# A planned instruction order with a reserve on VectorE's results and TensorE's operands

## The chip, the cores and the metric

The kernel runs on one core of a Trainium2 chip. The metric is the device time in microseconds of one execution; for the kernel before it is the median of three runs. A profiled execution gives the trace from which the views below come. The engines are named as the profile does: PE is TensorE (PEld its weight loads), DVE VectorE, ACT ScalarE, POOL GpSimd, SP SyncE, which issues nearly all transfers (SPq is its queue).

## What is computed

Four graph layers are applied to 32 independent graphs ("batches" in the kernel) of 512 nodes with 128 features, all in float32. Each layer normalizes x, applies a ReLU and adds a graph layer's result to x:

```python
h = jnp.maximum(_layernorm(x), 0.0);  x = x + L0(h, adj)   # degree-normalized aggregation, leaky relu
h = jnp.maximum(_layernorm(x), 0.0);  x = x + L1(h, adj)   # elu of three projections, aggregations by adj and its transpose, tanh
h = jnp.maximum(_layernorm(x), 0.0);  x = x + L2(h, adj)   # four inner layers with L2-normalized adj in both directions, tanh
h = jnp.maximum(_layernorm(x), 0.0);  x = x + L3(h, adj)   # message passing and a GRU cell
```

So each batch is a long chain of small matmuls with vector and scalar work between them, and the batches do not depend on each other.

## The kernel before

The kernel first records every operation of all 32 batches with an engine, an expected duration, what it reads and what it writes. Then a planner, at build time, plays the recorded operations through in order of expected time and so fixes for each engine the order in which its instructions are issued. On the chip each engine runs its list strictly in that order and waits where an operand has not arrived. The planner's view of how late a result is:

```python
class Plan:
    SIGNAL = {"PE": 0.2, "DVE": 0.13, "ACT": 0.14, "POOL": 0.06, "SP": 0.05, "AQ": 0.05}
    RESULT = {"PE": 0.0, "DVE": 0.125, "ACT": 0.13, "POOL": 0.05}
    LOAD = 0.1
    RATE, ALONE, TRANSFER, ISSUE = 400.0, 175.0, 1.5, 0.45
    ...
    def lag(self, o, n):          # from the start of o until n, which needs it, may start
        queued = o.engine == n.engine and o.engine in self.RESULT
        if queued:
            return o.us + self.RESULT[o.engine]
        return o.us + o.land + self.SIGNAL[o.engine] + self.LOAD * (n.engine == "PE")
```

`order()` keeps a ready queue for each engine. Of the ready operations it takes the one with the smallest key, a due time of its batch (batches are due `PERIOD` = 27 apart) less the length of the chain that still follows it. An operation that needs a buffer is held while too few are free, and newer batches have to leave some for older ones:

```python
new = [x for x in item[1].bufs if x.slot is None and x.kind in free]
older = item[1].batch - min(unfinished)
if any(len(free[x.kind]) < len([y for y in new if y.kind == x.kind])
       + older * self.kept.get(x.kind, 0) for x in new):
    held.append(item)
    continue
...
event(now + o.us + o.land + self.SIGNAL[e], "end", o)      # o's buffers may be given on
```

The kinds of buffers are "bank" (PSUM banks), "s2" (512 columns), "s4" and "s8"; the last argument says how many of each kind stay free for each older batch:

```python
plan = Plan(sb, psum, {"bank": 8, "s2": 32, "s4": 6, "s8": 10}, {"bank": 1, "s2": 6, "s4": 0, "s8": 1})
```

Loads of adjacency matrices and of x are marked `yields`: they are not issued while a turn through DRAM is under way.

Where the planner sees TensorE idle for longer than 0.7 us, filler products (`ps_idle`, 128 columns, results unused) are put in, `n = int(min(gap, cold) / COLD + max(gap - cold - 0.1, 0.0) / WARM)` of them with `COLD` = 0.428 and `WARM` = 0.2225; `cold` is spent in the first gap.

The operations that the text below names by their line of the kernel before (the lines of the changed kernel are one higher):

```python
# L530  x of a batch is loaded, 256 KB; L527 halves of adj (a) and its transpose (aT), 512 KB each
# L537, L539, L540  layernorm statistics of x (bn, mv, v) on DVE; L579 their power on POOL;
#                   L587 nb on DVE; L591 h = relu(...) on ACT, in four chunks
# L600 a [128, 512] matrix is transposed in 32x32 blocks (blk) on DVE;
# L609 four stores of 64 KB to DRAM (turn_...); L613 one load of 256 KB back (turned, or f4r);
# L633 ACT copies the turned matrix into place (hT, f); L899 DVE adds f4r to x
# L346 every ordinary product; L711 the products of seven() (ps_seven)
# L667 sd = products + bias on DVE; L689, L724, L737 the sums and differences around seven() on DVE
# L752, L832 row sums of a and sums of squares of a and aT on ACT
# L783 z from the first layer's products on DVE
# L805, L806, L808 rep = elu(...): exp on ACT, then two steps on DVE
# L854 a and aT are scaled by rows of norms on DVE (8 of 512 columns each batch)
# L883 f = tanh(...) on ACT, after each inner layer;  L957 the result is stored, 256 KB
aggregate(psi, rep, 0, aT)       # rep is the weight operand of the product with aT and with a
```

A matmul of n columns in the program appears as two records in the trace; `ps_t` transposes as one.

Of the kernel before, what the change touches and what calls it, by code (L numbers as in the profile page):

```python
# [96 lines left out]
class Plan:  # L97
# [2 lines left out]

    SIGNAL = {"PE": 0.2, "DVE": 0.13, "ACT": 0.14, "POOL": 0.06, "SP": 0.05, "AQ": 0.05}
    RESULT = {"PE": 0.0, "DVE": 0.125, "ACT": 0.13, "POOL": 0.05}

    LOAD = 0.1

# [51 lines left out]
    def lag(self, o, n):  # L161
# [6 lines that stand above are left out]
    def order(self):  # L168
# [13 lines left out]
        for o in self.ops:  # L182
            unfinished[o.batch] = unfinished.get(o.batch, 0) + 1
        queues, idle_at = {e: [] for e in self.SIGNAL}, dict.fromkeys(self.SIGNAL, 0.0)
        under_way = 0
        events, seq = [], 0

        def event(at, what, o=None):
            nonlocal seq
            seq += 1  # L190
            heapq.heappush(events, (at, seq, what, o))
# [5 lines left out]
        while events:  # L197
# [14 lines left out]
            for e, queue in queues.items():  # L212
# [24 lines left out]
                event(now + o.us, "idle")  # L237
                event(now + o.us + o.land + self.SIGNAL[e], "end", o)
                for n in o.next:
# [36 lines left out]
def gnn_stack(  # L276
# [13 lines left out]
    sb = ctx.enter_context(tc.tile_pool(name="sb", bufs=1))  # L290
    psum = ctx.enter_context(tc.tile_pool(name="psum", bufs=1, space=bass.MemoryType.PSUM))
    dram = ctx.enter_context(tc.tile_pool(name="dram", bufs=1, space=bass.MemoryType.DRAM))
    plan = Plan(sb, psum, {"bank": 8, "s2": 32, "s4": 6, "s8": 10}, {"bank": 1, "s2": 6, "s4": 0, "s8": 1})

    w_sb = const.tile([P, W_COLS], F32, name="w_sb")
    c_sb = const.tile([P, C_COLS], F32, name="c_sb")
# [716 lines left out]
```

## Time and profile before

| | |
|---|---|
| median of 3 runs | 2313.61 us (2312.37 to 2313.68) |
| span of the profiled execution | 2312.6 us, 28086 instructions |
| mean granted TensorE clock | 1.000 |
| DMA | 200.82 MB in 132334 packets, mean 87 GB/s |
| median time to landing: x, 256 KB | 5.3 us |
| median time to landing: half of aT, 512 KB | 5.2 us |
| median time to landing: stores of a turn, 64 KB; load back, 256 KB | 1.8 us; 2.7 us |

The page gives, for each engine, busy time with its share of the span and the number of instructions. In a view in order of time a line has start, duration, engine, source line, operation, output and inputs, shape and count, and in brackets the idle time of the engine before it and what ended it. In a view of waits a line has who waited for whom, the total in us, how many times, and the longest. Ends of matmuls are modelled, and matmuls are pipelined.

### The profile page before, as it was taken

The page shows a single profiled execution, that of the slowest core. Times are in us where ns is not written, and L with a number is a line of the kernel's source. Part 1 is how long each engine was busy: PE and PEld are TensorE (multiplying, and loading weights), DVE is VectorE, ACT ScalarE, POOL GpSimd, SP SyncE. Part 2 cuts the span into 40 slices and gives each one's busy share as a digit, 9 for nine tenths or more (in the row PEclk, how much of TensorE's full clock was granted, in tenths as well). Part 3 has the DMA queues.
Part 4 walks back from the last instruction along what each step waited for, and adds up shares of the span by engine and source line. Part 5 has one row for each costly group of instructions (what it writes and reads, how often), then busy time and mean ns, then how long its engine had stood idle before and what let it go on. Part 6 is the DMA issues. An engine that isn't in the chain of part 4 may idle for free.

```text
span 2312.6 us, 28086 instructions
## 1 busy us (share of the span) xinstructions
PE 2300.3 (99%) x9674; PEld 1448.6 (63%) x9674; DVE 1530.9 (66%) x4179; ACT 905.0 (39%) x1929; POOL 235.1 (10%) x171
## 2 busy tenths in 40 slices
PE   9999999999999999999999999999999999999999
PEld 7656666566666666666666656666566666666656
DVE  6646666677666776667766667766677666766656
ACT  7313434424344353433433434344343434434312
POOL 2000110101101011100101011010110101001100
PEclk9999999999999999999999999999999999999999
DMA  7001322323223232233232232222332322323201
GB/s 262 28 28 60 118 83 73 101 68 125 71 76 110 73 111 82 75 99 100 83 92 73 91 101 87 87 91 74 100 92 82 101 69 96 110 64 107 90 10 33
DMA packets 132334, 200.82 MB, mean 87 GB/s; under 512 B 18912, under 2 KB 79072, under 8 KB 132192
## 3 DMA queue, kind: packets, MB, share of 16 engines
q1 hardware_dynamic: 131904, 198.91, 27.2%
q8 instruction: 76, 1.25, 0.2%
q14 instruction: 66, 0.54, 0.1%
q10 hardware_dynamic: 288, 0.13, 0.0%
HBM read 160.05 MB, written 38.93 MB: 86 GB/s over the span
## 4 chain that ended last, share of the span: by engine, by line
PE 91%; DMA 4%; DVE 3%; SPq 0%; POOL 0%; ACT 0%; issue 0%; ACTq 0%; POOLq 0%
PE ps_agg L346 61%; PE ps_seven L711 11%; PE ps_sd L346 9%; PE ps_upd L346 4%; PE ps_gate L346 3%; DMA x<-in_x 1%; PE ps_msg L346 1%; PE ps_node L346 1%; PE ps_lin L346 1%; DMA turn_f4r<-blk 1%; DMA a<-in_adj 0%; DMA f4r<-turn_f4r 0%; POOL sc L579 0%; DVE blk L600 0%; DMA bounce<-inv 0%; DVE g L934 0%
## 5 line engine op out<-in xcount | busy, mean ns | idle before, releaser
L346 PE MATMUL ps_agg<-aT,sd 128*128 128x512 f32 x1024 | 505.5, 593 | 0.0
L346 PE MATMUL ps_agg<-a,sd 128*128 128x512 f32 x1024 | 492.8, 594 | 1.1 <-DVE sd L689 0.9
L579 POOL TENSOR_TENSOR sc<-v,neg_half 128x4 f32<-128x4 f32 (+1 forms) x127 | 176.5, 1390 | 1671.7 <-DVE v L540 1270.0
L591 ACT ACTIVATE h<-xr,nb,sc 128x128 f32<-128x128 f32 x384 | 158.3, 482 | 298.2 <-DVE nb L587 297.7
L346 PEld LDWEIGHTS ps_agg<-a,sd 128*128 128x128 f32 x1024 | 179.0, 191 | 149.6 <-issue 145.4
L346 PEld LDWEIGHTS ps_agg<-aT,sd 128*128 128x128 f32 x1024 | 181.5, 191 | 110.5 <-issue 102.0
L711 PEld LDWEIGHTS ps_seven<-t_sb,s 128*128 128x128 f32 x1140 | 168.8, 191 | 102.6 <-issue 89.7
L346 PE MATMUL ps_agg<-f,w_sb 128*128 128x512 f32 x448 | 230.2, 595 | 0.0
L346 PE MATMUL ps_sd<-w_sb,f 128*128 128x256 f32 x768 | 223.0, 380 | 0.0
L346 PEld LDWEIGHTS ps_sd<-w_sb,f 128*128 128x128 f32 x768 | 137.5, 191 | 115.5 <-issue 95.2
L711 PE MATMUL ps_seven<-t_sb,s 128*128 128x128 f32 x1140 | 178.4, 275 | 1.2 <-DVE s L689 1.2
L883 ACT ACTIVATE f<-ps_agg,cf_sb 128x512 f32<-128x512 f32 x128 | 87.5, 683 | 186.8 <-PE ps_agg L346 186.6
L667 DVE TENSOR_TENSOR sd<-ps_sd,rf_sb 128x512 f32<-128x512 f32 x128 | 87.6, 684 | 85.7 <-PE ps_sd L346 84.3
L346 PE MATMUL ps_agg<-aT,rep 128*128 128x512 f32 x256 | 131.4, 595 | 4.0 <-DVE rep L808 4.0
L346 PE MATMUL ps_agg<-a,rep 128*128 128x512 f32 x256 | 130.7, 592 | 0.0
L346 PE MATMUL ps_agg<-aT,msg 128*128 128x512 f32 (+1 forms) x264 | 130.1, 579 | 0.0
L711 PEld LDWEIGHTS ps_seven<-w_sb,f 128*128 128x128 f32 x512 | 77.0, 191 | 39.8 <-issue 32.5
L346 PE MATMUL ps_agg<-aT,h 128*128 128x256 f32 (+2 forms) x384 | 99.4, 381 | 0.6 <-ACT h L564 0.6
L346 PEld LDWEIGHTS ps_agg<-f,w_sb 128*128 128x128 f32 x448 | 77.9, 191 | 35.0 <-issue 29.7
L667 DVE TENSOR_TENSOR sd<-ps_sd,sd 128x512 f32<-128x512 f32 x64 | 43.7, 683 | 84.7 <-PE ps_sd L346 84.7
L832 ACT ACTIVATE sq<-aT 128x512 f32<-128x512 f32 x128 | 80.4, 628 | 35.9 <-DMA aT<-in_adjt 33.5
L737 DVE TENSOR_TENSOR ev<-ps_seven,ev 128x512 f32<-128x512 f32 x95 | 64.3, 677 | 44.4 <-PE ps_seven L711 44.2
(168 smaller groups left out, 3733.9 us busy)
## 6 DMA issues: line engine op xcount, KB each, us to landing
aT<-in_adjt SPq DMA_DIRECT2D x124, 512.0 KB, 5.2
a<-in_adj SPq DMA_DIRECT2D x62, 512.0 KB, 5.1
turn_turned<-blk SPq DMA_DIRECT2D x348, 64.0 KB, 1.8
turned<-turn_turned SPq DMA_DIRECT2D x87, 256.0 KB, 2.7
spaced<-bounce SPq DMA_DIRECT2D x32, 512.0 KB, 3.6
x<-in_x SPq DMA_DIRECT2D x32, 256.0 KB, 5.3
out<-xo SPq DMA_DIRECT2D x31, 256.0 KB, 2.1
turn_f4r<-blk SPq DMA_DIRECT2D x116, 64.0 KB, 1.8
```

What stands on the lines that cost most here:

```text
L346: op("PE", t_mm(n), lambda: nc.tensor.matmul(out_of(ps.ap()), lhs(), rhs(), start=start, stop=stop), reads, [ps], later=later)
L579: op("POOL", t_pow(n), lambda: nc.gpsimd.tensor_tensor(inv.ap()[:, :n], v8.ap()[:, :n], neg_half[:, :n], op=ALU.pow), [v8, NH], [(inv, {0})])
L591: op("ACT", t_act(D, 2), lambda c=c: nc.scalar.activation(h.ap()[:, c, :], xin.ap()[:, c, :], AF.Relu, bias=nb.ap()[:, c:c + 1], scale=inv ...
L667: op("DVE", t_tt(N), lambda ps=ps, h=h: nc.vector.tensor_add(sd.ap()[:, 2 * h:2 * h + 2, :], ps.ap().rearrange("p (j v) -> p j v", j=2), s ...
L711: op("PE", t_mm(D), lambda j=j: nc.tensor.matmul(ps.ap()[:, k * H + j * D:k * H + (j + 1) * D], lhs()[:, j * P:(j + 1) * P], rhs(), start= ...
L737: op("DVE", t_tt(N), lambda: nc.vector.tensor_add(ev.ap(), bank_b.ap()[:, None, :H].to_broadcast([P, 2, H]), ev.ap()), [bank_b, ev], [ev])
L832: op("ACT", 0.73, lambda c=c, s=s, m=m: nc.scalar.activation(sq.ap(), m.ap()[:, c, :], AF.Square, accum_out=stat.ap()[:, s * NC + c:s * NC ...
L883: op("ACT", t_act(N, 1), lambda ps=ps, i=i, f_new=f_new: nc.scalar.activation(f_new.ap(), ps.ap(), AF.Tanh, bias=cf_sb[:, i:i + 1]), [ps, ...
```

## The change

When the planner fixes the order, a result of DVE counts as seen by the other engines 0.25 us after its end instead of 0.13, and an operand of a matmul that comes from another engine or a transfer counts 0.25 us later instead of 0.1. Both are later than the results arrive, so that the order has a reserve where an instruction takes longer than the planner thought. With it the number of "s2" buffers that a newer batch leaves free for each older one goes from 6 to 5. The instructions themselves, their operands' shapes and the filler rule are the same; only the order, the buffers' places and the number of fillers can differ.

```diff
-    SIGNAL = {"PE": 0.2, "DVE": 0.13, "ACT": 0.14, "POOL": 0.06, "SP": 0.05, "AQ": 0.05}
+    SIGNAL = {"PE": 0.2, "DVE": 0.25, "ACT": 0.14, "POOL": 0.06, "SP": 0.05, "AQ": 0.05}
     RESULT = {"PE": 0.0, "DVE": 0.125, "ACT": 0.13, "POOL": 0.05}
 
-    LOAD = 0.1
+    LOAD = 0.25
...
-    plan = Plan(sb, psum, {"bank": 8, "s2": 32, "s4": 6, "s8": 10}, {"bank": 1, "s2": 6, "s4": 0, "s8": 1})
+    plan = Plan(sb, psum, {"bank": 8, "s2": 32, "s4": 6, "s8": 10}, {"bank": 1, "s2": 5, "s4": 0, "s8": 1})
```

## Prediction

> **What bounds the kernel now.** I read the page's busy times first, then TensorE's waits, then the waits of the engine that is named there, then single places in order of time. The page's first part:
>
> ```profile
> PE 2300.3 (99%) x9674; PEld 1448.6 (63%) x9674; DVE 1530.9 (66%) x4179; ACT 905.0 (39%) x1929; POOL 235.1 (10%) x171
> ```
>
> TensorE bounds, but its 99% hides how much is left. In order of time, its matmuls of 512 columns look like this:
>
> ```profile
> 1000.42 1.02 PE L346 MATMUL ps_agg<-a,rep 128*128 128x512 f32 x2
> 1001.28 1.02 PE L346 MATMUL ps_agg<-aT,sd 128*128 128x512 f32 x2
> ```
>
> Two records (one product in the program) start 0.86 us before the next two and are drawn 1.02 us long. So a record overlaps its successor by some 0.16 us, and a stall shows only with what exceeds that. I therefore counted from start to start. The spacing of records that wait for nothing is 0.429 us at 512 columns (3322 records), 0.324 at 384 (128), 0.216 at 256 (1188) and 0.112 at 128 (5027): 1425 + 41 + 257 + 563 = 2286 us. From the first start (1.4 us) to the last there are 2308 us, so 21 us are stalls; another 3 us follow the last matmul. Of the 2286, 9.6 us are the 86 filler records (43 filler products). So 2277 us are real work that the change leaves alone, and all it can win lies in 21 + 10 us.
>
> Where the 21 us are, by the matmul's last-arriving operand: 6.5 us lie in the first 50 us, 14.5 net in the rest, nearly none in the last 100. TensorE's waits name the cause:
>
> ```profile
> PE ps_agg L346 <- DVE rep L808: 4.0, 6, 0.9
> PE ps_seven L711 <- DVE s L689: 1.2, 3, 0.7
> PE ps_agg L346 <- DVE sd L689: 0.9, 4, 0.2
> ```
>
> Start to start, after the first 50 us: L808 4.4 us at 6 places, L689 5.2 us at 21, the tanh of L883 1.5 us at 13 (0.12 each), hT (L633) 0.5 us at 2: 11.6 us. The other 4.4 us are steps of about 0.1 us with no late operand.
>
> Why is VectorE late? Its own waits, and one place of each kind:
>
> ```profile
> DVE xr L899 <- DMA f4r<-turn_f4r: 17.5, 14, 2.5
> DVE bn L537 <- DMA x<-in_x: 10.3, 10, 3.7
> ```
>
> ```profile
> 1421.65 0.29 DVE L537 BATCH_NORM_STATS2 bn<-x 128x6 f32<-128x128 f32 x1 [1.13 <-DMA x<-in_x]
> 1421.86 0.67 DVE L808 TENSOR_TENSOR rep<-rep,sd 128x512 f32<-128x512 f32 x1
> ```
>
> ```profile
> 1422.68 1.10 PE L346 MATMUL ps_agg<-aT,rep 128*128 128x512 f32 x2 [0.94 <-DVE rep L808]
> ```
>
> A statistic of the next x stands in VectorE's queue ahead of rep; x has not landed; rep waits behind it, and TensorE with it. The other kind is a late f4r (the matrix turned through DRAM):
>
> ```profile
> 1625.50 0.69 DVE L899 TENSOR_TENSOR xr<-xr,f4r 128x512 f32<-128x512 f32 x1 [2.48 <-DMA f4r<-turn_f4r]
> ```
>
> ```profile
> 1628.94 0.94 PE L711 MATMUL ps_seven<-t_sb,s 128*128 128x128 f32 x6 [0.68 <-DVE s L689]
> ```
>
> So the named releaser is VectorE, but behind both kinds stands a transfer.
>
> **What the Trainium skill says.** "Perfetto Trace Analysis", section "Identifying the Most-Contended Engine": matmul busy share is a poor measure of the distance to the limit; the overlap above agrees. The same page, "DVE / Act Engine Instruction": the end shown is the write's acknowledgement, and the semaphore must still spread. Here stalled matmuls start 0.055 us after the end shown for L689's results and 0.147 us after L808's. Section "Tensor Engine Instruction" calls VectorE a strict FIFO: the x place agrees. "TensorE: Matmul & The Clock Gate", "What's actually happening": TensorE is throttled after idling some 3.4 us. The granted clock is 1.000 here and the longest stall 1.1 us, so no speed is at stake.
>
> **The change part by part.** No matmul, VectorE or ScalarE instruction changes its work. In the planner, a result of VectorE counts as seen 0.12 us later by every other engine, and any operand of a matmul from another engine or a DMA 0.15 us later (so VectorE to TensorE 0.27 us); and a newer batch need leave only 5 small buffers per older batch. Only orders move, so I read both orders, and for each matmul that waits I counted the matmul time (spacings above) between the matmul that feeds the VectorE or ScalarE work and this one, less that work's own durations (0.687 us for L667 from the trace, and so on). What is left must pay the hand-overs:
> - L808 to the aggregate: 15 of 63 places had 0.51 us or less. After: one in the first batch at 0.15, all others 0.76 or more, mostly 1.41.
> - L667 to the aggregate: 40 of 190 had 0.34 to 0.39; after, all but one have 0.65 or more.
> - L689 to the aggregate: least 0.49, a quarter below 0.78; after 0.72 and 1.01.
> - L883's tanh to the next product: 43 of 63 had about 0.4; after 0.63 at least.
>
> Two distances between issue and use matter more. x's load stood 2.6 to 2.8 us of matmul time ahead of its statistics, while the page has 5.3 us to landing; after, 9.4 us. f4r: from the VectorE transposition to its use 7.15 or 7.38 us; measured it needs 6.7 to 8.4; after, 9.13. The order also settles differently: before, it repeats every two batches (141.2 us of matmul time), after, every batch (70.65).
>
> Removed: L808 4.4 + L689 5.2 + L883 1.5 + L633 0.5 = 11.6 us. The 4.4 us of small steps stay.
>
> Added, fillers: 49 products instead of 43. Six by 0.223 us (two records of 0.112) is 1.3 us. Two of them stand before products in the first 42 us that wait anyway (0.5 to 0.75 us of stall behind the fillers), and cost nothing. The other four are new, near 250 us, where a tanh has too little beside it: 0.9 us.
>
> Added, transfers: the tightest path is now h1 turned through DRAM. From transposition to the product that uses hT the order leaves 7.45 us in every batch (before 7.41 and 7.67 in turn). Measured: 6.5 to 6.8 us until ScalarE starts its copy when nothing interferes, 0.62 us of copy, 0.06 us of hand-over: 7.2 to 7.5. And in the new order f4r's way back and the output store are issued just ahead of its way back, 256 KB each. The data of 256 KB take about 1.1 us on the queue alone and some 0.7 us in a busy stretch, so I allow 0 to 0.3 us of stall a batch, 0.1 on average: 27 x 0.1 = 2.7 us. For what I overlook in start and end, 1 us.
>
> Sum: 2313.6 - 11.6 + 0.9 + 2.7 + 1.0 = 2306.6. I say 2306.5 us, a gain of 0.3%.
>
> **Rivals.** (1) The reserve moves nothing that matters, because matmul work sets the cadence in both orders (141.2 us for two batches, 70.65 for one): 2314 us, with the fillers. For it speaks the 99%; against it that both transfers behind the stalls get 2 to 7 us more time. (2) The transfers gathered in one window become a stall in every batch. A period of one batch means that a site 0.5 us short costs 27 x 0.5 = 13 us, more than all that is won: 2317 us. For it speaks hT at 7.45 against 7.2 to 7.5, and from the first issue of a to the first product of h, 13.1 us, where the trace has h ready at about 12.0 to 13.0; against it, that in the old order 7.41 us for hT cost only 0.5 us in all. (3) All late operands vanish and nothing takes their place: 2313.6 - 11.6 + 0.9 = 2303 us; if the small steps went too, 2299.
>
> **Range and chances.** The floor of 2299 and rival (2) bound it. I hold the gain likelier than not, rival (2) in full at a tenth: 2299 to 2313 us. Two per cent is 46 us. All stalls and fillers together are 31, so faster by over 2% is excluded by the sum (0.01 for a mistake in it); slower by as much needs 1.7 us more stall in each of 27 batches (0.01).
>
> **What would show it.** In the changed profile: 98 filler records; TensorE's waits on L808 under 1 us in all, on L689 under 1 us; VectorE's wait for x nearly gone and for f4r under 5 us instead of 17.5; 2277 us of real work as before; any new wait should be on ScalarE's hT (L634 there), once in each batch. I am wrong if L808 and L689 still cost over 4 us start to start though x and f4r are early (then VectorE's queue, not the transfers, made them late), or if hT or h costs over 0.3 us in most batches.

## The result, and the profile after

The changed kernel takes 2325.86 us (median; 2321.68 to 2331.6), the kernel before, run beside it on the same chip, 2313.64 us (2311.85 to 2315.32). The ratio is 1.0054, with a 95% interval of 1.0040 to 1.0068: the change costs 12 us where the prediction had a gain of 7, and the time lies outside its range of 2299 to 2313 us.

The profiled execution of the changed kernel is its fastest: its span is 2319.9 us against 2312.6 before. So the trace shows 7.3 us of the 12, and the rest has to be read from the experiments. First the page's busy times, after:

```profile
PE 2298.2 (99%) x9686; PEld 1448.7 (62%) x9686; DVE 1521.4 (66%) x4179; ACT 898.9 (39%) x1929; POOL 206.5 (9%) x171
```

TensorE's busy time is lower than before (2300.3) although the kernel is slower, and 99% says nothing again. The chain of work that ended last says more; here its line of shares by engine, before and then after:

```profile
PE 91%; DMA 4%; DVE 3%; SPq 0%; POOL 0%; ACT 0%; issue 0%; ACTq 0%; POOLq 0%
```

```profile
PE 81%; DVE 7%; DMA 6%; ACT 3%; issue 2%; SPq 1%; POOL 0%; ACTq 0%; DVEq 0%
```

Ten points of the chain have left TensorE for other engines, transfers and the queue. TensorE's waits after (who waited for whom, total us, times, longest):

```profile
PE ps_sd L347 <- ACT hT L634: 15.2, 20, 1.4
PE ps_idle L963 <- POOL ident masks.py:199: 1.4, 1, 1.4
PE ps_agg L347 <- ACT h L565: 0.6, 1, 0.6
PE ps_agg L347 <- DVE diag L764: 0.5, 1, 0.5
PE ps_agg L347 <- DVE sd L668: 0.2, 1, 0.2
```

The three groups behind VectorE's rep and s have vanished, and one new group stands in their place: the products that use h1 turned (hT) wait for ScalarE's copy of it. VectorE's waits for transfers changed as follows:

```profile
DVE diag L764 <- DMA aT<-in_adjt: 35.7, 29, 2.1
DVE bn L538 <- DMA x<-in_x: 4.4, 2, 3.7
DVE xr L900 <- DMA f4r<-turn_f4r: 0.7, 2, 0.5
```

f4r fell from 17.5 us to 0.7, x from 10.3 to 4.4, of which 3.7 are the very first load. The new wait for aT (in nearly every batch) reaches TensorE only once, with 0.5 us (0.4 before).

Start to start, as the prediction counts, the books are these. Spacing without stalls: 2286.8 us before, 2288.2 after (12 more filler records). Stalls, net: 21.1 before, 27.0 after. Another 4.7 us lie ahead of the first product and behind the last in both, and the sums are the two spans, 2312.6 and 2319.9. Of the 27.0 us, 19.2 stand behind hT at 24 places, 0.8 us each; before it was 0.5 us. Everything else fell from 20.6 to 7.8.

One such place. The queue of SyncE in order of time, first the kernel before, then after (start, duration, what is issued):

```profile
1408.25 0.40 SPq L957 DMA_DIRECT2D out<-xo  x1
1409.66 0.34 SPq L613 DMA_DIRECT2D f4r<-turn_f4r  x1
1410.06 1.85 SPq L609 DMA_DIRECT2D turn_turned<-blk  x4
1413.82 0.34 SPq L613 DMA_DIRECT2D turned<-turn_turned  x1
```

```profile
1412.61 1.76 SPq L610 DMA_DIRECT2D turn_turned<-blk  x4
1414.60 0.34 SPq L614 DMA_DIRECT2D f4r<-turn_f4r  x1
1414.99 0.42 SPq L958 DMA_DIRECT2D out<-xo  x1
1415.80 0.32 SPq L614 DMA_DIRECT2D turned<-turn_turned  x1
1416.17 0.97 SPq L528 DMA_DIRECT2D aT<-in_adjt  x2
```

Before, the result's store and f4r's way back went out 5.6 and 4.2 us ahead of h1's way back. After, all three go out within 1.2 us. ScalarE and TensorE at the same place:

```profile
1420.81 0.62 ACT L634 COPY hT<-turned 128x512 f32<-128x512 f32 x1 [7.12 <-DMA turned<-turn_turned]
```

```profile
1421.48 1.78 PE L347 MATMUL ps_sd<-w_sb,hT 128*128 128x256 f32 x7 [1.07 <-ACT hT L634]
```

From the issue of the way back (1415.80) to the copy it is 5.0 us. Over the 25 batches in the middle the median is 4.53 us; before it was 2.62. The store itself takes longer as well (median us from issue to landing, last column, before and after):

```profile
out<-xo SPq DMA_DIRECT2D x31, 256.0 KB, 2.1
```

```profile
out<-xo SPq DMA_DIRECT2D x31, 256.0 KB, 3.2
```

### The profile page after: what moved, and what is told of

It reads as the page before. It is cut to its first block, busy times and chain, and to the rows that moved or that the text cites. A ratio compares the mean times of both kernels' runs of the same rounds, so it can differ in the third digit from the quotient of the medians.

```text
span 2319.9 us, 28193 instructions
## 1 busy us (share of the span) xinstructions
PE 2298.2 (99%) x9686; PEld 1448.7 (62%) x9686; DVE 1521.4 (66%) x4179; ACT 898.9 (39%) x1929; POOL 206.5 (9%) x171
## 4 chain that ended last, share of the span: by engine, by line
PE 81%; DVE 7%; DMA 6%; ACT 3%; issue 2%; SPq 1%; POOL 0%; ACTq 0%; DVEq 0%
PE ps_agg L347 55%; PE ps_sd L347 9%; PE ps_seven L712 9%; DMA turned<-turn_turned 4%; PE ps_upd L347 4%; DMA turn_turned<-blk 2%; ACT h L592 1%; PE ps_gate L347 1%; PE ps_msg L347 1%; PE ps_node L347 1%; PE ps_lin L347 1%; SPq L610 1%; DVE g L935 1%; DVE bn L538 1%; DVE blk L601 1%
## 5 line engine op out<-in xcount | busy, mean ns | idle before, releaser
L347 PE MATMUL ps_agg<-aT,sd 128*128 128x512 f32 x1024 | 492.6, 592 | 0.2 <-DVE sd L668 0.2
L347 PE MATMUL ps_agg<-a,sd 128*128 128x512 f32 x1024 | 485.8, 593 | 0.0
L580 POOL TENSOR_TENSOR sc<-v,neg_half 128x4 f32<-128x4 f32 (+1 forms) x127 | 149.1, 1174 | 1816.0 <-DVE v L541 1340.3
L347 PEld LDWEIGHTS ps_agg<-aT,sd 128*128 128x128 f32 x1024 | 186.8, 190 | 155.6 <-issue 142.8
L347 PE MATMUL ps_sd<-w_sb,f 128*128 128x256 f32 x768 | 217.8, 380 | 0.0
L712 PEld LDWEIGHTS ps_seven<-t_sb,s 128*128 128x128 f32 x1140 | 158.7, 191 | 50.3 <-issue 34.2
L712 PE MATMUL ps_seven<-t_sb,s 128*128 128x128 f32 x1140 | 166.3, 275 | 0.0
L634 ACT COPY hT<-turned 128x512 f32<-128x512 f32 x58 | 35.9, 618 | 193.6 <-DMA turned<-turn_turned 193.0
L920 ACT ACTIVATE mT<-ps_agg 128x512 f32<-128x512 f32 x31 | 18.5, 596 | 218.9 <-PE ps_agg L347 218.9
L855 DVE TENSOR_TENSOR a<-a,rows 128x512 f32<-128x512 f32 x128 | 86.1, 674 | 6.8 <-PE ps_agg L347 6.8
```

Of the source, the lines that this page charges most:

```text
L347: op("PE", t_mm(n), lambda: nc.tensor.matmul(out_of(ps.ap()), lhs(), rhs(), start=start, stop=stop), reads, [ps], later=later)
L580: op("POOL", t_pow(n), lambda: nc.gpsimd.tensor_tensor(inv.ap()[:, :n], v8.ap()[:, :n], neg_half[:, :n], op=ALU.pow), [v8, NH], [(inv, {0})])
L634: op("ACT", t_act(N), lambda: nc.scalar.copy(hT.ap().rearrange("p (c a r) -> p c a r", c=NC, a=NC), turned_cols(t)), [t], [hT])
L712: op("PE", t_mm(D), lambda j=j: nc.tensor.matmul(ps.ap()[:, k * H + j * D:k * H + (j + 1) * D], lhs()[:, j * P:(j + 1) * P], rhs(), start= ...
L855: op("DVE", t_tt(N), lambda m=m, c=c, s=s: nc.vector.tensor_mul(m.ap()[:, c, :], m.ap()[:, c, :], rows.ap()[:, s, :]), [(m, {c}), rows], [ ...
```

## The experiments

In all tables "way" is the median from the issue of h1's way back to the start of ScalarE's copy in the 25 middle batches, "stalls of hT" what TensorE loses there start to start (with the number of places), and "all" the net stalls of the whole span. Source lines in the profiles shift with the edits.

### Which of the two transfers does it

The changed kernel's orders are kept, and in the 25 batches single transfers are moved in SyncE's queue (the edit in short, not its code):

```diff
+ for back in ways_back_of_h1:                 # with f4r's way back and the store just ahead of it
+     for o in (the two transfers ahead):
+         if kind(o) in which:                 # e1: the store; e2: f4r's way back; e3: both
+             move o directly behind back
```

> The changed kernel with one thing moved: in the transfers' queue the store of the result (256 KB) goes behind the way back of h1's turn (256 KB) instead of ahead of it, in the 25 batches where both f4r's way back and this store stand ahead of it. All other engines' orders are the same. Theory A (transfers queue up: each of the two 256 KB ahead costs hT about 0.9 us): hT's way from issue to copy falls from 4.5 to about 3.6 us, TensorE's stalls for hT from 19 us to under 4 us, time about 2310 us. Rival B (the store alone does it, a write to DRAM in front of a read): way falls to 2.7 us, stalls to nothing, about 2306 us. Rival C (the loads of aT and x issued right behind take the bandwidth): way stays over 4.2 us, time stays about 2325 us.

> The changed kernel with f4r's way back moved behind h1's way back, the store stays ahead. Theory A: hT's way about 3.6 us, stalls for hT under 4 us, about 2310 us, as with the store moved. Rival B (the store alone): no gain, 2325 us. Rival C (the loads behind): 2325 us. f4r itself is about 1 us later, which its 9.1 us of room should bear: VectorE's wait for it under 10 us in all.

> The changed kernel with both f4r's way back and the store moved behind h1's way back. Theory A: hT's way 2.7 us, no stalls for hT beyond 1 us in all, time 2306 us (2313.6 less the 11.6 us of stalls that the new order removed, plus the fillers, plus what f4r's delay costs), so faster than the kernel before. Rival B: the same as with the store moved alone. Rival C: still 2325 us.

| run | ahead of h1's way back | way | stalls of hT | all | time | ratio (95%) |
|---|---|---|---|---|---|---|
| after | f4r, store | 4.53 | 18.7 (23) | 27.0 | 2325.86 | 1.0054 (1.0040 to 1.0068) |
| e1 | f4r | 3.38 | 4.3 (3) | 11.6 | 2304.94 | 0.9966 (0.9954 to 0.9978) |
| e2 | store | 2.75 | 0.7 (2) | 29.7 | 2323.84 | 1.0048 (1.0033 to 1.0063) |
| e3 | nothing | 2.67 | 1.0 (2) | 32.4 | 2324.81 | 1.0053 (1.0038 to 1.0068) |

Moving the store alone turns a loss of 12 us into a gain of 8. Moving f4r's way back frees hT even more (2.75 us), but then f4r itself is late: VectorE's wait for it was expected under 10 us and is 42.8. The waits of e2, VectorE's and TensorE's:

```profile
DVE xr L914 <- DMA f4r<-turn_f4r: 42.8, 26, 2.9
```

```profile
PE ps_agg L360 <- DVE rep L823: 14.9, 25, 1.2
```

This is the mechanism that the prediction had found in the kernel before (a late transfer holds up VectorE's queue, and TensorE with it), now in nearly every batch; there a late f4r stood before s, here it stands before rep. e3 goes the same way: f4r 44.9 us, rep 16.8 in 25 places. Two transfers want the same place in the queue, and the one sent behind pays. What was expected of each alone did not come: neither an equal share for the two nor "the store alone" describes 0.1 for the store, 0.7 for f4r and 1.9 for both. That transfers issued behind the way back slow it by themselves is refuted: with f4r and the store directly behind it (e3) it took 2.67 us, and the changed kernel's turns of h3, with nothing near them, 2.65. Whether the two halves of aT, 0.37 us behind, add to the delay of a way back that has f4r and the store ahead was not tested.

### The planner does it itself, and the queue it goes through

One word in the changed kernel has the store wait while a turn is under way (e5); or the store is issued from ScalarE's queue instead of SyncE's (e7):

```diff
- op("SP", 0.4, lambda: nc.sync.dma_start(out[b], xo.ap()), [xo], [], kb=256)
+ op("SP", 0.4, lambda: nc.sync.dma_start(out[b], xo.ap()), [xo], [], kb=256, yields=True)    # e5
+ op("SP", 0.4, lambda: nc.scalar.dma_start(out[b], xo.ap()), [xo], [], kb=256)               # e7
```

> The changed kernel with one word more: the store of the result is also held back while a turn through DRAM is under way. The order stays that of the changed kernel but for the store, which now stands behind h1's way back, and 45 of 4867 matmuls near the end. Theory (two 256 KB transfers ahead of hT's way back cost it 1.8 us, f4r's alone 0.7, which the order can bear): as with the store moved by hand, 2305 us, within 3; stalls for hT under 5 us. Rival (the gain of the store moved by hand was a chance of that one program): over 2312 us.

> The changed kernel with the store of the result issued from ScalarE's queue at the same place in the order, so that it isn't in SyncE's queue ahead of hT's way back. Theory (SyncE's queue hands its transfers' data on in turn, so what counts is what stands ahead in that queue): hT's way back falls to about 3.4 us as with the store moved behind it, stalls under 6 us, about 2306 us. Rival (the data paths are shared by all queues, whatever the queue): the way stays over 4.2 us and the time about 2325 us.

| run | way | stalls of hT | all | time | ratio (95%) |
|---|---|---|---|---|---|
| e5 | 3.39 | 2.8 (4) | 10.0 | 2304.39 | 0.9952 (0.9940 to 0.9964) |
| e7 | 4.79 | 25.8 (25) | 35.6 | 2329.18 | 1.0060 (1.0046 to 1.0074) |

e5 is faster than both kernels and has the lowest median here, though e1 (2304.94) and e14 below (2304.87) lie within the noise of it; its chain has 96% on TensorE. e7 shows that the harm is not done in SyncE's queue: the Trainium skill ("DMA: Bandwidth & Descriptors", section "Issuing engines are not separate DMA queues") says that transfers of all issuing engines run on the same 16 DMA engines and interleave, and here the other queue made it slightly worse.

### By which rule the delay should have been worked out

Three more edits of the changed kernel's queue: half of the store (128 KB) stays, the other half goes behind (e13); the store goes ahead of f4r's way back (e14); the store goes behind and the next x's load, also 256 KB, takes its place (e15).

```diff
  f4r<-turn_f4r              # after         e13: f4r, 1/2 out, turned, 1/2 out
- out<-xo                    #               e14: out, f4r, turned
  turned<-turn_turned        #               e15: f4r, x, turned, out
```

> The changed kernel, with the result's store cut in two: 128 KB stay between f4r's way back and h1's way back, 128 KB are issued just behind h1's. Measured so far from the issue of h1's way back to ScalarE's copy: nothing ahead 2.65 us, the store alone 2.75 (0.9 us ahead), f4r alone 3.38 (1.19 us ahead), both 4.53. Theory (a queue: each transfer keeps the paths for its own time, so the delay is the sum of these times less the head start): from f4r alone 1.19 + 0.73 = 1.92 us, from the store alone 0.9 + 0.1 = 1.0; for both 1.92 + 1.0 - 1.19 = 1.73, so 4.38 (measured 4.53). With half the store 1.92 + 0.5 - 1.19 = 1.23, so 3.9 us. The way from transposition to use may then take some 8.5 us without a stall, so stalls of hT of 1 to 8 us, about 2308 us. Rival (the two disturb each other, or either part of the store does the harm whole): 4.4 us or more, stalls of hT above 12 us, 2318 us or more. Second rival (the delays add up singly, 0.73 + under 0.1): 3.4 us, 2304 to 2305.

> The changed kernel, with the result's store issued ahead of f4r's way back instead of behind it (both still ahead of h1's way back). Queue theory: the order of the two does not matter; if the store goes out 1.2 us and f4r 0.8 us ahead, -1.19 + 1.0 + 1.92 = 1.73: 4.4 us from issue to copy, stalls of hT of 15 us or more and 2320 us or more; f4r itself comes some 0.4 us later or more. Rival (a load back that stands directly ahead matters, a store does not): f4r with 0.8 us head start alone gives 2.65 + 1.92 - 0.8 = 3.8 us, about 2308 us.

> The changed kernel, with the result's store issued just behind h1's way back and the next x's load (256 KB as well, but from DRAM like the two ways back) put in the store's place between f4r's and h1's way back. Without anything in that place h1's way took 3.38 us from issue to copy, with the store there 4.53, with half the store 4.0, with the store ahead of both 2.97. If bytes between the two are what counts: 4.3 us or more, stalls of hT of 15 us or more, 2320 us or more. If a store between two loads is what counts: a load in its place costs less than half of the 1.15 us that the store cost, 3.9 us or less, stalls of hT under 8 us, 2304 to 2309 us.

| run | ahead, in order | way | stalls of hT | all | time | ratio (95%) |
|---|---|---|---|---|---|---|
| e13 | f4r, half the store | 4.09 | 9.7 (20) | 18.6 | 2314.24 | 1.0005 (0.9998 to 1.0012) |
| e14 | store, f4r | 2.97 | 3.3 (4) | 9.7 | 2304.87 | 0.9965 (0.9952 to 0.9978) |
| e15 | f4r, x | 3.93 | 7.4 (15) | 16.1 | 2311.38 | 0.9995 (0.9986 to 1.0004) |

e14 is the cleanest single proof that this place in the queue is the cause: nothing but two neighbours change places, and 21 us go. Its queue at one place, the wait that is left, and the store's time to landing:

```profile
1408.60 0.36 SPq L969 DMA_DIRECT2D out<-xo  x1
1409.14 0.34 SPq L624 DMA_DIRECT2D f4r<-turn_f4r  x1
1409.64 0.33 SPq L624 DMA_DIRECT2D turned<-turn_turned  x1
```

```profile
PE ps_sd L357 <- ACT hT L645: 2.6, 4, 1.1
```

```profile
out<-xo SPq DMA_DIRECT2D x31, 256.0 KB, 2.0
```

The simple queue (each transfer keeps the paths for a time of its own, in order) hit e13's way roughly (3.9 expected, 4.09 measured; its time, about 2308 expected, not) and falls with e14, where it wanted 4.4 and 2.97 was measured; the rival there wanted 3.8 and falls too. So the place of the store counts. Whether it is the order or the distances is not separated: in e14 f4r goes out 0.50 us ahead of h1's way back instead of 1.19, the store 1.04 instead of 0.80. Bytes count as well: a load in the store's place costs 3.93 - 3.38 = 0.55 us, the store 1.15. e15 lies just above its line between the two theories, so neither holds alone. One may read it as half of the harm from 256 KB more between the two ways back and half from its being a store behind a load; that split is argued, not shown. The store's own landing points the same way (2.0 us ahead of the loads, 3.2 between them, 3.6 behind both in e1). Nor are the paths full while h1's way back waits: behind f4r alone (e1, the same batch as above) the DMA engines moved 236, 90, 138 and 402 GB/s in the first four stretches of 0.8 us after its issue. So for some 1.6 us they ran far below the rate that they reached just after. Why that is so, and why a store behind a load is slow, is not shown by these runs.

### The two halves of the change

Each part of the change alone: the allowances with 6 buffers kept (e4), 5 buffers kept with the old allowances (e8), and one allowance each (e11, e12):

```diff
  # e4:   DVE 0.25, LOAD 0.25, kept 6      e8:   DVE 0.13, LOAD 0.1,  kept 5
  # e11:  DVE 0.25, LOAD 0.1,  kept 6      e12:  DVE 0.13, LOAD 0.25, kept 6
```

> The reserve alone: both allowances as in the changed kernel, but 6 small buffers left free for each older batch as before. The order has 86 filler products instead of 49 (before: 43) and repeats every three batches; no place has both f4r and the store ahead of hT's way back. Theory A: no stalls for hT of note; 43 more fillers than before by 0.223 us are 9.6 us, less the 11.6 us of stalls before, plus what the planner's gaps really are: about 2313 us, within 5 us. Rival (the allowances themselves make VectorE's or hT's path late): over 2325 us.

> The other half of the change alone: 5 small buffers left free instead of 6, without the allowances. 47 fillers; the order repeats every two batches, and in every second one f4r's way back and the store stand ahead of hT's way back with 7.61 us of room, f4r 7.4 in the others. Theory (the two transfers ahead are what costs): hT stalls by 0.6 to 0.8 us at 13 places, some 9 us, on top of stalls behind VectorE of 5 to 12 us as before: 2317 to 2324 us. Rival (the allowances are what makes hT late): hT's stalls under 3 us, 2313 us.

> The allowance for VectorE's results alone (0.25); operands of TensorE at 0.1 and 6 small buffers kept, as before. The planner sees TensorE idle in many more places and puts in 252 filler products, 209 more than before: 209 x 0.223 = 46.6 us of matmul time that is issued whatever the operands do. Theory: they cost nearly all of it, less what they fill of real waits (at most some 15 us): 2340 to 2362 us. Rival: the fillers stand where TensorE really waits and cost little: under 2325.

> The allowance for TensorE's operands alone (0.25); VectorE's results at 0.13 and 6 small buffers kept, as before. 254 filler products, 211 more than before: 211 x 0.223 = 47.1 us. Theory as for the other allowance alone: 2340 to 2362 us. Rival: under 2325.

| run | filler products | all stalls | time | ratio (95%) |
|---|---|---|---|---|
| before | 43 | 21.1 | | |
| e4, both allowances | 86 | 14.8 | 2318.53 | 1.0026 (1.0016 to 1.0037) |
| e8, 5 kept | 47 | 27.8 | 2322.94 | 1.0036 (1.0022 to 1.0049) |
| e11, VectorE's allowance | 252 | 20.6 | 2361.94 | 1.0207 (1.0189 to 1.0226) |
| e12, operands' allowance | 254 | 28.4 | 2369.04 | 1.0238 (1.0219 to 1.0257) |

The reserve itself does what it is for: e4 loses 6 us of stalls. TensorE's waits for rep and for s and sd of L689 fall from 6.1 us to 0.9, although VectorE waits 20.6 us for x and 8.8 for f4r there. It pays 43 more filler products for it (43 x 0.223 = 9.6 us) in an order that repeats only after three batches, and its time lies just above the range expected (2313 within 5). The 5 buffers alone bring the coincidence of the transfers: in 13 batches of e8 f4r's way back and the store stand ahead of h1's, its way takes 4.70 us there, and TensorE's waits read

```profile
PE ps_sd L346 <- ACT hT L633: 13.0, 13, 2.3
```

The single allowances are dominated by filler products. 209 x 0.223 = 46.6 us and 211 x 0.223 = 47.1 us are just what the spacing without stalls grew by (to 2333.6 and 2334.1 us). The fillers take next to nothing from real waits: the stalls fell by 0.5 us in e11 and rose by 7 in e12, which put it above the range expected. So the effects of the parts do not add up to the whole; each setting makes another order.

### Was the late x the cause before?

The kernel before, with x's load ahead of what stood in front of it. e6 moved it ahead of the preceding turn, where there was one; e9 ahead of the two halves of a:

```diff
- turned, a, a, x               # before, every second batch
+ turned, x, a, a               # e9
- turn_turned x4, turned, x     # before, the other batches
+ x, turn_turned x4, turned     # e6
```

> The kernel before with one transfer moved: in every second batch x's load is issued ahead of the turn that it stood behind, so that 8.7 us of matmul time lie before its statistics instead of 2.6; every other engine's order is the same. Theory (the stalls behind rep came from a late x, not from a late VectorE): TensorE's stalls behind rep fall from 4.4 us to under 1 us, VectorE's wait for x from 10.3 us to under 5, time about 2309.5 us. Rival (hand-overs to TensorE are too short in the old order whatever the transfers do, so only a reserve helps): stalls behind rep stay over 3 us, time stays 2313 us.

> The kernel before, with x's load moved ahead of the two halves of the adjacency matrix that stood directly in front of it (this is so in every second batch, the ones whose x was late), about 0.9 us earlier in the queue; every other order is the kernel's before. Theory of the prediction (x lands late, its statistics hold up rep in VectorE's queue, and rep holds up TensorE): x lands in some 3 us instead of 6.4, VectorE's wait for x falls from 10.3 us to under 2, TensorE's stalls behind rep from 4.4 us to under 1, and the time falls by 3 to 4.5 us to about 2310. Rival (rep is late because VectorE has too much to do ahead of it, whatever x does): the wait for x goes but rep's stalls stay above 3 us and the time stays at 2313 to 2314.

e6: 2314.97 us, ratio 1.0003 (0.9994 to 1.0011). It tells nothing of the theory: the late x are those behind the two halves of a (landing 5.6 us after issue in the median, up to 6.5 in the middle of the run; behind a turn 3.0), and these e6 had left in their place (rep still costs 5.2 us). e9 moves just these, and every x then lands some 2.9 us after issue: 2308.81 us, ratio 0.9977 (0.9969 to 0.9984). TensorE's waits and VectorE's wait for x in e9:

```profile
PE ps_seven L726 <- DVE s L704: 1.6, 3, 0.6
PE ps_idle L977 <- POOL ident masks.py:199: 1.4, 1, 1.4
PE ps_agg L360 <- DVE sd L704: 1.1, 5, 0.2
PE ps_agg L360 <- DVE diag L778: 0.8, 1, 0.8
PE ps_agg L360 <- ACT h L578: 0.6, 1, 0.6
```

```profile
DVE bn L551 <- DMA x<-in_x: 4.6, 3, 3.8
```

No rep is left in the list, VectorE's wait for x fell from 10.3 to 4.6 us (3.8 of it at the start), and all stalls from 21.1 to 16.0: 5.1 us for one load sent 0.9 us earlier. The rival (VectorE has too much to do ahead of rep) falls. Late f4r was not touched (18.4 us), and s still makes TensorE wait.

### Without a reserve

The kernel before with 5 buffers kept, the store yielding, and a turn's transfers counted at 1.8 us instead of 1.5:

```diff
-    RATE, ALONE, TRANSFER, ISSUE = 400.0, 175.0, 1.5, 0.45
+    RATE, ALONE, TRANSFER, ISSUE = 400.0, 175.0, 1.8, 0.45
```

> The kernel before with three settings of the planner changed and both allowances at their old values: 5 small buffers kept, the store of the result waits while a turn through DRAM is under way, and a turn's transfers count as 1.8 us instead of 1.5. 50 filler products; the order repeats after every batch; the order leaves 7.84 us from the transposition of h1 to the use of hT and 8.10 for f4r. If late transfers alone were what the reserve had to cure, this does the same without any reserve: 2303 to 2306 us, with stalls of 11 to 13 us. If VectorE's results need the reserve for themselves: stalls behind rep and s as in the kernel before, 2310 or more.

2308.62 us, ratio 0.9978 (0.9969 to 0.9987), all stalls 14.2 us. It lies between the two expectations. f4r's wait is gone (0.5 us at one place), and of the groups behind VectorE 0.2 us is left for rep and one place of 1.0 for the results of seven(). The two longest new stalls are 1.2 us each, one behind ScalarE at 46 us and that one at 356 us. VectorE's wait for x even grew to 66.8 us (29 places) and costs TensorE nothing that shows. So such a wait does not harm by itself; that it harms only where rep stands behind it without room is argued. The stalls behind VectorE can go without a reserve, f4r's because f4r came in time, x's although x came later. As three settings changed at once, the share of each is not known.

## Why the prediction was wrong

- **What bounds the kernel, and what the change removes: right.** 98 filler records, no wait on rep, under 1 us on s, f4r's wait 0.7 us, x's gone but for the start. Predicted removal 11.6 us, 0.5 of it hT's; everything but hT fell by 12.8. That a transfer stood behind VectorE's lateness was shown for x by e9 (5.1 us; the step had 4.4). For f4r, e2 and e3 show that a late one does it, by making rep late; that it was f4r behind s in the kernel before was not tested alone (f4r and s stay together in e9 and go together in the changed kernel and in e10).
- **The step that failed** is the term for the transfers added: "I allow 0 to 0.3 us of stall a batch, 0.1 on average: 27 x 0.1 = 2.7 us". It was 0.75 us on average in 25 batches, from nothing to 1.6, 18.7 us in all, and 19.2 with one place more. The place, the engine and the cause were named as they came; the size was wrong sevenfold. The sign of being wrong that the text gave (hT over 0.3 us in most batches) came in 19 of the 25.
- **Why it was mis-sized.** "7.2 to 7.5" for the need was measured in the order before, where the store and f4r had 4 us and more of head start. In the new order the need is 3.92 us to the issue, 4.53 of way, 0.62 of copy and 0.05 of hand-over: 9.12. The delay was estimated from the data time of one transfer (0.7 to 1.1 us), with most of it taken as past by then; measured, the two cost 1.9 us together, and e1 and e14 show that it is not a matter of data time alone.
- **A second error hid part of the first.** The room was put at 7.45 us, counted from matmuls in the order. From the start of the transposition to the use e1 and e14, where hT is rarely late, have 8.38 us in the median, 0.9 us more than counted. 9.12 - 8.38 is 0.74 us, about what was measured. In the kernel before the trace has 7.70 us in every second batch and 9.52 in the others, for a need of 3.94 + 2.62 + 0.62 + 0.05 = 7.23 us, so the tight batches had some 0.4 us to spare. "In the old order 7.41 us for hT cost only 0.5 us in all" was therefore no argument: the change made the room larger, and the need grew by more (from 7.23 to 9.12).
- **Rival (2) is what happened**, with its mechanism (a period of one batch turns one short site into 25) and nearly its size (13 us expected, 18.7 measured). The text gave it a tenth and ended the range below its 2317 us, though it had itself found both transfers ahead of the tightest path. A rival for which the order already shows the coincidence belongs inside the range.
- **The rest of the sum held.** Without the hT term it is 2306.6 - 2.7 = 2303.9 us; with the store out of the way e5 took 2304.39, e14 2304.87 and e1 2304.94.
- **The sum had no term for the spread of the runs**: of the 12.2 us of the median, the traced execution shows 7.3. That hT makes the other 5 is likely (its way spread from 3.6 to 5.4 us among the batches of the trace), but it was not traced.

## What to carry to other kernels

When an order is regenerated, look first at what now stands directly ahead of each transfer that an engine will wait for: a 256 KB store that costs 0.1 us alone cost 1.2 us between two loads, in every batch. Send a store that nobody waits for ahead of the loads or behind the last urgent one, and measure the room of a path from start to use where nothing waits, not from the planned order. A fixed reserve on results made an order that bears late transfers here (e4), but that is another order, with fillers and neighbours of its own; the late load itself, sent 0.9 us earlier, gave 5 us.

## What the runs showed of the hardware that was not expected

- Two neighbours in one queue, a store of 256 KB and a load of 256 KB ahead of a load that is waited for: store first, 2.97 us to the copy; load first, 4.53. The store alone ahead gave 2.75, the load alone 3.38, nothing 2.65 to 2.67.
- Transfers issued behind a load of 256 KB, even 0.4 us behind it and 1 MB or more in all, hardly slowed it: with nothing ahead it landed in 2.70 us with two halves of aT behind it and in 2.56 without (medians, before), in 2.68 with two halves of a and one of aT behind it and in 2.63 without (after). This fits the Trainium skill ("DMA: Bandwidth & Descriptors", section "Two DMAs through the same engine are not ordered"), by which the descriptors of one queue of one DMA engine start in order.
